# Which last convolutions wait for the last mixing, and in which order an inverse transform emits its steps

## The chip, the cores and the metric

The kernel runs on one core of one Trainium2 chip. The metric is device time in microseconds (us) of one execution; a lower number is better. All arithmetic is float32 (a few transforms split a float32 number into two reduced-precision parts and add the two products).

## The reference

The input is `x` of shape (4, 64, 256, 256): 4 batches, 64 channels, images of 256 x 256. Four layers run one after the other:

- Layers 0, 1 and 3 are the same kind of layer, a long convolution per channel plus a scaled copy of the input: `y = irfft2(rfft2(x) * k_f)[:256, :256] + x * bias`. The filter of a channel is an outer product of one vector along the rows and one along the columns (`k = einsum('ijk,imk->ijmk', hx, hy)`), so a two-dimensional convolution is two one-dimensional ones, and each of these is a product with a triangular Toeplitz matrix.
- Layer 2 is a Haar wavelet layer:

```python
f1 = haar2d(x)
for i in range(2):
    f3 = f1 * v[i]
    f4 = einsum('bchw,oc->bohw', f3, conv_w[i])   # mixes the 64 channels
    acc = acc + sign(f4) * relu(abs(f4) - tau[i])
y = haar2d(acc, inverse=True) + x
```

The mixing needs all 64 channels of a batch; everything else works on one channel alone.

## The kernel before

**The work of one batch** falls into three parts, and each has a function in the kernel.

1. `convolutions(b, ticks)`: for each channel, the convolutions of layers 0 and 1 (tiles `a0`, `y0`, `a1`, `y1`) and then the forward Haar transform along rows and columns (`sd`, `pz`, `co`). The coefficients go to memory as `coef`, and the input of the wavelet layer is saved as `keep`. A *contraction* (`contract`, lines 167 and 168) multiplies a 256 x 256 image with a triangular Toeplitz matrix; it appears as four matmuls in the code and eight in the trace. A convolution takes two contractions: the first into bank `pa`, copied by ScalarE to `a` (`first`, line 176), the second into bank `py`, where VectorE adds the bias term and writes `y` (`second`, line 189).
2. `mixing(b, start, n_act)`: 64 groups `g`. Each loads four rows of coefficients of all channels, mixes the channels on TensorE (`px`, line 308), scales (`f`, lines 325 and 327), shrinks (`mag`, lines 333, 335 and 340) and adds into `z` (line 344).
3. `inverse(b, start, put_off)`: for each channel `c`, one tick apart, `fetch` loads the saved `keep` as `r` (line 359) and lets ScalarE gather the channel out of `z` as `zc` (line 361); `rows` makes four matmuls into bank `pw` (lines 368 and 369), then ScalarE rounds (`w`, line 371) and VectorE takes the rest (line 372); `cols` makes the column transform into bank `pu` (line 381), then VectorE adds `r` (`t`, line 385) and unpacks the pairs (`u`, lines 388 and 389). `u` is the input of layer 3. The *last convolution* of a channel is layer 3: `first`, `second` and the write to the output (`last`, line 403).

**Order of the work.** The kernel does not run these functions one after the other. Each stage of each unit is noted with `at(tick, place, run, unit)`; at the end all notes are sorted by tick, then by place, then by the order of noting, and called in that order. A scheduler below may still shift an instruction by a few places, above all loads. On each engine the instructions then stand in one order. `stream` gives stage `s` of a unit the tick `tick + s` and the place `-s`, so that within a tick a later stage (of an earlier unit) comes first.

**How the parts lie beside each other.** The mixing of batch `b` runs for 67 ticks beside `convolutions(b + 1)`, whose 64 units are spread evenly over it (`spread`). Then the inverse of batch `b` runs for 64 ticks beside the rest of those convolutions. Batch 3 has no next batch, so its mixing would have nothing beside it. Therefore the third batch (`b == B - 2`) is treated differently: its inverse computes no last convolution but writes `u` to memory (`late`), and `convolution(2, ticks)` loads the 64 images again beside the last mixing and computes the last convolutions there. And 20 of the 64 units of `convolutions(3)` are moved from the third mixing into the third inverse:

```python
            ticks = spread(ahead, end + 2)
            if b == B - 2:
                ticks = spread(ahead, end, 44) + spread(end, end + 49, 20)
```

**Buffers.** All banks `pa`, `py`, `pw`, `pu`, `pz` come from one pool of four in PSUM (`psm`); the Toeplitz tiles `t` from a pool of five; `u` and `y0` share a pool of three (`y`); `y3`, the final result of a channel, and `co` share one of two; `r` and the mixing's `f` share one of three. Loads and the write of `coef` are issued on SyncE (SP), the writes of `keep`, `late` and the output on ScalarE's queue.

Of the kernel before, what the change touches and what calls it, by code (L numbers as in the profile page):

```python
# [9 lines left out]
F32 = mybir.dt.float32  # L10
# [6 lines left out]
B, C, S, EMB, ORD = 4, 64, 256, 33, 64  # L17
P = 128
# [19 lines left out]
def conv_seq_kernel(ctx, tc, x, fz, fw, bias, decay, haar, haar_row, factors, vt, taut, wmix, out):  # L38
# [14 lines left out]
    nc = tc.nc  # L53

    const = ctx.enter_context(tc.tile_pool(name="const", bufs=1))
    dram = ctx.enter_context(tc.tile_pool(name="dram", bufs=1, space=DRAM))
# [93 lines left out]
    sd = zpool.tile([P, 8, 2, 2, P], F32, name="sd")  # L150
    keep = [dram.tile([C, P, 2, 2, P], F32, name=f"keep{b}") for b in range(B)]
    coef = [dram.tile([2, C, P, S], F32, name=f"coef{b}") for b in range(B)]
    late = dram.tile([C, P, 2, S], F32, name="late")

    def toeplitz(layer, c, name):

        t = tp.tile([P, 2, S], F32, name=name, tag="toep")
        nc.sync.dma_start(t, ap(pads[layer], c * 2 * ROW, [[1, P], [ROW, 2], [1, S]]))
        return t
# [45 lines left out]
    def at(tick, place, run, unit):  # L205
        events.append((tick, place, len(events), run, unit))

    def stream(stages, ticks):

        for unit, tick in enumerate(ticks):  # L210
            for s, stage in enumerate(stages):
                if stage is not None:
                    at(tick + s, -s, stage, unit)

    def convolutions(b, ticks, in_parts=False):

        st = {}

        def load(c):
            xt = io.tile([P, 2, S], F32, name=f"x_{b}_{c}", tag="in", bufs=4)  # L220
            nc.sync.dma_start(xt, x[b, c].rearrange("(k p) w -> p k w", p=P))
            st[c] = {"x": xt, 0: toeplitz(0, c, f"t0_{b}_{c}")}

        last_second = second(b, st, "a1", 1, "y0", "y1", "res")

        def pairs(c):
            last_second(c)
            v = st.pop(c)["y1"].rearrange("p k (w e) -> p k w e", e=2)
            t = sd[:, c % 8]
            nc.vector.tensor_add(t[:, :, 0, :], v[:, :, :, 0], v[:, :, :, 1])  # L230
            nc.vector.tensor_sub(t[:, :, 1, :], v[:, :, :, 0], v[:, :, :, 1])  # L231
            nc.scalar.dma_start(keep[b][c], t)

        def levels(steps):
            def run(n):
                t = sd[:, n % 2 * 4 : n % 2 * 4 + 4]
                for step in steps:
                    v = t[:, :, :, 0, :].rearrange("p c k (w e) -> p (c k) w e", e=2 * step)
                    even, odd = v[:, :, :, 0], v[:, :, :, step]
                    nc.vector.tensor_sub(odd, even, odd)  # L240
                    nc.vector.scalar_tensor_tensor(even, even, 2.0, odd, ALU.mult, ALU.subtract)

            return run

        parts = {}

        def split(c):

            w = parts[c] = mx.tile([P, 2, 2, S], F32R, name=f"sp_{b}_{c}", tag="f4")
            t = sd[:, c % 8].rearrange("p k e w -> p k (e w)")  # L250
            nc.scalar.copy(w[:, 0], t)
            nc.vector.tensor_tensor(w[:, 1], t, w[:, 0].bitcast(F32), ALU.subtract)

        def down(c):
            ps = bank(f"pz_{b}_{c}")
            flat = "p k w -> p (k w)"
            if in_parts:
                for i in range(2):
                    nc.tensor.matmul(
                        ps.rearrange(flat), hbr, parts[c][:, i].rearrange(flat), start=(i == 0), stop=(i == 1)  # L260
                    )
            else:
                nc.tensor.matmul(
                    ps.rearrange(flat), hbt, sd[:, c % 8].rearrange("p k e w -> p (k e w)"), start=True, stop=True
                )
            t = io.tile([P, 2, S], F32, name=f"co_{b}_{c}", tag="co", bufs=BUFS["co"])
            nc.scalar.copy(t, ps)
            nc.sync.dma_start(coef[b][:, c].rearrange("k p w -> p k w"), t)

        stream(  # L270
            [load, first(b, st, "x", 0, "a0"), second(b, st, "a0", 0, "x", "y0", "y", ahead=1), first(b, st, "y0", 1, "a1"), pairs],
            ticks,
        )
        for n in range(C // 4):
            end = ticks[4 * n + 3] + 4
            for s, steps in enumerate([(1,), (2, 4), (8, 16, 32, 64)]):
                at(end + 1 + s, 1, levels(steps), n)
            for j in range(4):
                if in_parts:
                    at(end + 3 + j, 2, split, 4 * n + j)  # L280
                at(end + 4 + j, 2, down, 4 * n + j)
        return ticks[-1] + 11
# [68 lines left out]
    def inverse(b, start, put_off):  # L351

        st = {}

        def fetch(c):
            if c == 0:
                butterfly(b)
            r = mx.tile([P, 2, 2, P], F32, name=f"r_{b}_{c}", tag="f", bufs=3)
            nc.sync.dma_start(r, keep[b][c])
            a = mx.tile([P, 2, 2, P], F32, name=f"zc_{b}_{c}", tag="mag")  # L360
            nc.scalar.copy(a, z[:, :, :, c].rearrange("p h (i k) -> p h k i", k=2))  # L361
            st[c] = {"r": r, "z": a}

        def rows(c):
            a = st[c]["z"]
            ps = psm.tile([P, 2, 2, P], F32, name=f"pw_{b}_{c}", tag="mm")
            for m in range(2):
                nc.tensor.matmul(ps[:, m, 0, :], a[:, 0, m, :], hsinv, start=True, stop=True)  # L368
                nc.tensor.transpose(ps[:, m, 1, :], a[:, 1, m, :], ident)  # L369
            w = mx.tile([P, 2, 2, 2, P], F32R, name=f"w_{b}_{c}", tag="f4")  # L370
            nc.scalar.copy(w[:, 0], ps)  # L371
            nc.vector.tensor_tensor(w[:, 1], ps, w[:, 0].bitcast(F32), ALU.subtract)
            st[c]["w"] = w
            if not put_off:
                st[c][2] = toeplitz(2, c, f"t2_{b}_{c}")

        def cols(c):
            ps = psm.tile([P, 2, 2, P], F32, name=f"pu_{b}_{c}", tag="mm")
            flat = "p m e w -> p (m e w)"
            for i in range(2):  # L380
                nc.tensor.matmul(  # L381
                    ps.rearrange(flat), hb, st[c]["w"][:, i].rearrange(flat), start=(i == 0), stop=(i == 1)
                )
            t = io.tile([P, 2, 2, P], F32, name=f"t_{b}_{c}", tag="res", bufs=BUFS["res"])
            nc.vector.scalar_tensor_tensor(t, st[c]["r"], 0.5, ps, ALU.mult, ALU.add)  # L385
            u = io.tile([P, 2, S], F32, name=f"u_{b}_{c}", tag="y", bufs=BUFS["y"])
            v = u.rearrange("p m (w e) -> p m w e", e=2)
            nc.vector.tensor_add(v[:, :, :, 0], t[:, :, 0, :], t[:, :, 1, :])
            nc.vector.tensor_sub(v[:, :, :, 1], t[:, :, 0, :], t[:, :, 1, :])
            st[c]["u"] = u  # L390

        stages = [None, fetch, rows, cols]
        if put_off:
            stages.append(lambda c: nc.scalar.dma_start(late[c], st.pop(c)["u"]))
        else:
            stages += last(b, st)
        stream(stages, range(start - 1, start - 1 + C))

    def last(b, st):
        return [  # L400
            first(b, st, "u", 2, "a3"),
            second(b, st, "a3", 2, "u", "y3", "co"),
            lambda c: nc.scalar.dma_start(out[b, c].rearrange("(k p) w -> p k w", p=P), st.pop(c)["y3"]),
        ]

    def convolution(b, ticks):

        st = {}

        def load(c):  # L410
            u = io.tile([P, 2, S], F32, name=f"v_{b}_{c}", tag="in", bufs=4)
            nc.sync.dma_start(u, late[c])
            st[c] = {"u": u, 2: toeplitz(2, c, f"t2_{b}_{c}")}

        stream([load, *last(b, st)], ticks)


    def spread(begin, end, n=C):
        return [begin + i * (end - begin - 1) // (n - 1) for i in range(n)]

    groups = S // 4
    ready = convolutions(0, range(C), in_parts=True)
    ahead = C
    start = ready + 3
    for b in range(B):
        mixing(b, start, 8 if b + 1 < B else 6)
        end = start + groups + 3
        if b + 1 < B:
            ticks = spread(ahead, end + 2)
            if b == B - 2:  # L430
                ticks = spread(ahead, end, 44) + spread(end, end + 49, 20)
            ready = convolutions(b + 1, ticks)
        else:
            convolution(b - 1, spread(start - 2, end + 2))
        inverse(b, end, put_off=b == B - 2)

        start = max(end + C, ready + 3)
        ahead = start - 3
# [112 lines left out]
```

## Time and profile before

| | us |
|---|---|
| three runs | 3121.33, 3124.04, 3125.69 |
| median | 3124.04 |
| the profiled execution, its own time | 3127.37 |
| its span in the profile | 3125.6 |

| stretch of the profile (us from the start) | length, us |
|---|---|
| filters, then the convolutions of batch 0 | 486.0 |
| mixing 0 from its first `f` to its last `z`, then inverse 0 (486.0 to 1190.4) | 704.4 |
| mixing 1, inverse 1 (1190.4 to 1944.5) | 754.1 |
| mixing 2, inverse 2 (1944.5 to 2587.7) | 643.2 |
| mixing 3, inverse 3 (2587.7 to 3125.6) | 537.9 |

A stretch begins with the first scaling (`f`, line 325) of its mixing. The granted TensorE clock is 0.996 of full speed in the mean, so the clock hardly plays a part. In the profile PE is the matmuls of TensorE, PEld its weight loads, DVE is VectorE, ACT is ScalarE. [...] neighbours overlap in the record; what an instruction costs TensorE is the distance from its start to the next one's start.

### The profile page before, as it was taken

Reading aid. Unit: us, or ns where it says so; the run is one execution under the profiler, and the core shown is the slowest. Engines: PE = TensorE matmul, PEld = TensorE weight load, DVE = VectorE, ACT = ScalarE, POOL = GpSimd, SP = SyncE. Lnnn points to the kernel's source line nnn. Section 1 sums busy time; section 2 is a strip of 40 time slices with the busy share of each in tenths; the row PEclk is TensorE's granted clock in tenths of the full one; section 3 lists DMA queues with packets and bytes.
Section 4 is the critical chain, followed back from the end, with each engine's and each line's share of the span. In section 5 each row is a group of like instructions: output and inputs, shape, how many; then the busy total and the mean of one; then the engine's idle time right before and its main releaser. Section 6 shows DMA issues by size and latency. Waiting matters only on the chain. (4 is left out here: it accounts for less than half of the span.)

```text
span 3125.6 us, 50721 instructions
## 1 busy us (share of the span) xinstructions
PE 3010.4 (96%) x16944; PEld 2622.0 (84%) x16944; DVE 2526.0 (81%) x4453; ACT 1923.9 (62%) x4054; POOL 0.2 (0%) x4
## 2 busy tenths in 40 slices
PE   5999999999999999999999999999998989999999
PEld 3999988888888998888888899888887768888998
DVE  6676668989986777988887676999987889998776
ACT  1333336777765555766675555778774557887554
POOL 0000000000000000000000000000000000000000
PEclk9999999999999999999999999999999999999999
DMA  4778776666667776666666777666667877886776
GB/s 121 218 228 233 230 228 205 202 195 188 199 200 217 211 210 188 196 204 194 203 201 207 217 211 203 190 187 186 191 206 232 254 241 236 239 232 210 211 211 180
DMA packets 555864, 649.82 MB, mean 208 GB/s; under 512 B 39793, under 2 KB 440532, under 8 KB 555476
## 3 DMA queue, kind: packets, MB, share of 16 engines
q1 hardware_dynamic: 439460, 493.44, 55.8%
q10 hardware_dynamic: 116144, 153.13, 13.6%
q8 instruction: 137, 2.24, 0.3%
q14 instruction: 123, 1.01, 0.1%
HBM read 426.67 MB, written 219.74 MB: 207 GB/s over the span
## 5 line engine op out<-in xcount | busy, mean ns | idle before, releaser
L167 PE MATMUL py<-t,a 128*128 128x256 f32 x3072 | 927.4, 384 | 25.5 <-ACT a L176 23.9
L176 ACT COPY a<-pa 128x512 f32<-128x512 f32 x768 | 458.6, 598 | 603.7 <-PE pa L168 487.1
L168 PEld LDWEIGHTS py<-t,a 128*128 128x128 f32 x3072 | 584.1, 190 | 79.4
L327 ACT ACTIVATE f<-px,vt 128x64 f32<-128x64 f32 x1920 | 424.2, 331 | 299.8 <-DVE f L325 292.0
L167 PEld LDWEIGHTS py<-t,a 128*128 128x128 f32 x3072 | 486.6, 191 | 128.8 <-issue 64.5
L168 PE MATMUL py<-t,a 128*128 128x128 f32 x3072 | 590.5, 274 | 0.0
L308 PE MATMUL px<-wb,f 128*128 128x256 f32 x2048 | 496.1, 380 | 5.4 <-ACT f L327 3.6
L308 PEld LDWEIGHTS px<-wb,f 128*128 128x128 f32 x2048 | 365.1, 191 | 46.3 <-ACT f L327 6.2
L385 DVE SCALAR_TENSOR_TENSOR t<-r,pu 128x512 f32<-128x512 f32 x256 | 175.9, 687 | 213.9 <-PE pu L381 207.4
L167 PE MATMUL pa<-t,y 128*128 128x256 f32 x1024 | 310.0, 385 | 27.3 <-DVE y L189 26.5
L335 DVE TENSOR_TENSOR mag<-mag,vt 128x1024 f32<-128x1024 f32 x256 | 312.3, 1220 | 29.4 <-ACT mag L333 27.6
L167 PE MATMUL pa<-t,x 128*128 128x256 f32 x1024 | 307.1, 382 | 8.6 <-DMA t<-pad 8.6
L340 DVE SCALAR_TENSOR_TENSOR mag<-mag,f 128x1024 f32<-128x1024 f32 x256 | 311.7, 1217 | 0.8
L333 ACT ACTIVATE mag<-f 128x1024 f32<-128x1024 f32 x256 | 283.8, 1108 | 9.6 <-DVE z L344 6.5
L361 ACT COPY zc<-z 128x512 f32<-128x512 f32 x256 | 282.0, 1103 | 8.0 <-DVE z L199 6.5
L334 ACT ACTIVATE f<-f 128x1024 f32<-128x1024 f32 x256 | 272.1, 1063 | 10.7 <-DVE sd L231 3.5
L371 ACT CAST w<-pw 128x512 fp32r<-128x512 f32 x256 | 150.1, 586 | 196.7 <-PE pw L369 177.3
L189 DVE SCALAR_TENSOR_TENSOR y<-y,bsb,py 128x512 f32<-128x512 f32 x256 | 190.2, 743 | 90.3 <-PE py L168 90.0
L189 DVE SCALAR_TENSOR_TENSOR y<-x,bsb,py 128x512 f32<-128x512 f32 x256 | 190.3, 743 | 53.4 <-PE py L168 53.3
L167 PE MATMUL pa<-t,u 128*128 128x256 f32 x768 | 229.7, 381 | 1.9 <-PE py L168 1.0
L168 PEld LDWEIGHTS pa<-t,x 128*128 128x128 f32 x1024 | 195.4, 191 | 26.7
L168 PEld LDWEIGHTS pa<-t,y 128*128 128x128 f32 x1024 | 195.3, 191 | 26.7
(65 smaller groups left out, 4342.9 us busy)
## 6 DMA issues: line engine op xcount, KB each, us to landing
t<-pad SPq DMA_DIRECT2D x768, 256.0 KB, 3.9
x<-in_x SPq DMA_DIRECT2D x256, 256.0 KB, 3.9
keep<-sd ACTq DMA_DIRECT2D x256, 256.0 KB, 3.2
coef<-co SPq DMA_DIRECT2D x256, 256.0 KB, 2.9
f<-coef SPq DMA_DIRECT2D x256, 256.0 KB, 3.8
r<-keep SPq DMA_DIRECT2D x256, 256.0 KB, 3.0
out_y<-y ACTq DMA_DIRECT2D x256, 256.0 KB, 3.6
late<-u ACTq DMA_DIRECT2D x64, 256.0 KB, 3.6
```

The lines of the kernel that those rows point to most:

```text
L167: nc.tensor.matmul(ps[:, m, :], src[:, 0, m * P : (m + 1) * P], t[:, ::-1], start=True, stop=False)
L168: nc.tensor.matmul(ps[:, m, P:], src[:, 1, m * P : (m + 1) * P], t[:, : P - 1 : -1], start=False, stop=True)
L176: nc.scalar.copy(a, ps)
L189: nc.vector.scalar_tensor_tensor(y, s[res], bsb[:, layer, c : c + 1], ps, ALU.mult, ALU.add)
L308: nc.tensor.matmul(ps[:, h, q, :], f[:, q, h * P : (h + 1) * P], wb.rearrange("p r n -> p (r n)"), start=True, stop=True,)
L327: nc.scalar.mul(f4[:, j], px[:, j], scale(g, 0)[:, j : j + 1])
L333: nc.scalar.activation(mag, f4, AF.Abs)
L334: nc.scalar.activation(f4, f4, AF.Sign)
L335: nc.vector.tensor_sub(mag, mag, over(g, 1, 16))
L340: nc.vector.scalar_tensor_tensor(mag, mag, 0.0, st[g]["f4"], ALU.max, ALU.mult)
L361: nc.scalar.copy(a, z[:, :, :, c].rearrange("p h (i k) -> p h k i", k=2))
L385: nc.vector.scalar_tensor_tensor(t, st[c]["r"], 0.5, ps, ALU.mult, ALU.add)
```

## The change

- `put_off` is no longer a yes or no for a whole batch but a set of channels: 2, 5, 8, ... 62, which is 21 of 64. In the inverses of batches 0, 1 and 2 these 21 channels write `u` to `late`; the other 43 make their last convolution in place. `late` grows to hold all batches.
- Beside the last mixing, `convolution` now computes 63 last convolutions, 21 of each of the first three batches, instead of 64 of the third.
- The 64 units of `convolutions(3)` are spread over the third mixing as in the batches before; none is left for the third inverse.
- The stages of an inverse get places of their own. Within a tick the order was: write, `second`, `first`, `cols`, `rows`, `fetch`. It becomes: `rows` (-9), `cols` (-8), `first` (-7), `second` (-6), write (-5), then the convolution and mixing stages of the tick, with `fetch` at place -1 among them. The ticks of the stages stay as they are. This holds for all four inverses, the last one too, which puts nothing off.

```diff
-    late = dram.tile([C, P, 2, S], F32, name="late")
+    late = dram.tile([B, C, P, 2, S], F32, name="late")
...
-            if not put_off:
+            if c not in put_off:
                 st[c][2] = toeplitz(2, c, f"t2_{b}_{c}")
...
-        stages = [None, fetch, rows, cols]
-        if put_off:
-            stages.append(lambda c: nc.scalar.dma_start(late[c], st.pop(c)["u"]))
-        else:
-            stages += last(b, st)
-        stream(stages, range(start - 1, start - 1 + C))
+        ends = last(b, st)
+        for c in range(C):
+
+            at(start + c, -1, fetch, c)
+            at(start + c + 1, -9, rows, c)
+            at(start + c + 2, -8, cols, c)
+            if c in put_off:
+                at(start + c + 3, -5, lambda c: nc.scalar.dma_start(late[b, c], st.pop(c)["u"]), c)
+            else:
+                for s, stage in enumerate(ends):
+                    at(start + c + 3 + s, s - 7, stage, c)
...
-    def convolution(b, ticks):
-
-        st = {}
-
-        def load(c):
-            u = io.tile([P, 2, S], F32, name=f"v_{b}_{c}", tag="in", bufs=4)
-            nc.sync.dma_start(u, late[c])
-            st[c] = {"u": u, 2: toeplitz(2, c, f"t2_{b}_{c}")}
-
-        stream([load, *last(b, st)], ticks)
+    def convolution(which, ticks):
+
+        for (b, c), tick in zip(which, ticks):
+            st = {}
+
+            def load(c, b=b, st=st):
+                u = io.tile([P, 2, S], F32, name=f"v_{b}_{c}", tag="in", bufs=4)
+                nc.sync.dma_start(u, late[b, c])
+                st[c] = {"u": u, 2: toeplitz(2, c, f"t2_{b}_{c}")}
+
+            for s, stage in enumerate([load, *last(b, st)]):
+                at(tick + s, -s, stage, c)
...
+    put_off = range(2, C, 3)
...
-            ticks = spread(ahead, end + 2)
-            if b == B - 2:
-                ticks = spread(ahead, end, 44) + spread(end, end + 49, 20)
-            ready = convolutions(b + 1, ticks)
+            ready = convolutions(b + 1, spread(ahead, end + 2))
         else:
-            convolution(b - 1, spread(start - 2, end + 2))
-        inverse(b, end, put_off=b == B - 2)
+            convolution(
+                [(i, c) for i in range(B - 1) for c in sorted(put_off)], spread(start - 2, end + 2, (B - 1) * len(put_off))
+            )
+        inverse(b, end, put_off if b + 1 < B else ())
```

## The prediction

> **What bounds the kernel now.** The page's first part comes first, then its slices.
>
> ```profile
> PE 3010.4 (96%) x16944; PEld 2622.0 (84%) x16944; DVE 2526.0 (81%) x4453; ACT 1923.9 (62%) x4054; POOL 0.2 (0%) x4
> ...
> PE   5999999999999999999999999999998989999999
> ...
> DMA  4778776666667776666666777666667877886776
> ```
>
> TensorE is the bound nearly everywhere; its share dips at slices 31 and 33. The window sums say which stage that is: mixing 1, inverse 1, mixing 2, inverse 2, mixing 3, inverse 3, in this order.
>
> ```profile
> 1190.40:1661.80 471.40, 463.68 (x2485) 398.30 (x2484) 414.19 (x691) 323.49 (x808) 0.00 (x0) 1.00 0.66 197
> 1661.80:1944.50 282.70, 282.19 (x1746) 253.96 (x1746) 196.06 (x373) 151.66 (x216) 0.00 (x0) 1.00 0.71 212
> 1944.50:2324.10 379.60, 368.24 (x1930) 312.16 (x1929) 357.24 (x569) 298.26 (x761) 0.00 (x0) 1.00 0.64 191
> 2324.10:2587.70 263.60, 231.08 (x1287) 189.82 (x1285) 203.04 (x433) 140.48 (x201) 0.00 (x0) 0.96 0.76 242
> 2587.70:2867.30 279.60, 271.48 (x1458) 239.42 (x1457) 274.33 (x321) 242.15 (x572) 0.00 (x0) 1.00 0.79 233
> 2867.30:3125.60 258.30, 249.78 (x1586) 228.81 (x1584) 176.47 (x324) 140.88 (x195) 0.00 (x0) 1.00 0.68 198
> ```
>
> The columns are length, then busy time of PE, PEld, DVE and ACT, clock, DMA share, GB/s. Only inverse 2 leaves TensorE idle by a lot (231 of 264 busy, weight loads 190). The waits inside it name the cause:
>
> ```profile
> PE pa L167 <- DVE y L189: 20.2, 14, 4.3
> PE pu L381 <- DVE w L372: 5.1, 7, 3.0
> PE pu L381 <- ACT w L371: 2.6, 6, 0.7
> ```
>
> Last, the timeline in the middle of inverse 0 shows one tick:
>
> ```profile
> 1063.62 0.69 DVE L385 SCALAR_TENSOR_TENSOR t<-r,pu 128x512 f32<-128x512 f32 x1 [1.01 <-PE pu L381]
> ...
> 1064.08 0.60 PE L167 MATMUL py<-t,a 128*128 128x256 f32 x2
> ...
> 1064.34 0.59 ACT L371 CAST w<-pw 128x512 fp32r<-128x512 f32 x1 [0.54 <-PE pw L369]
> 1064.34 0.43 DVE L388 TENSOR_TENSOR u<-t 128x256 f32<-128x256 f32 x1
> ...
> 1065.02 0.68 DVE L372 TENSOR_TENSOR w<-pw,w 128x512 fp32r<-128x512 f32 x1
> ...
> 1065.39 0.60 PE L167 MATMUL pa<-t,u 128*128 128x256 f32 x2
> ...
> 1067.17 0.38 PE L368 MATMUL pw<-hrow,zc 128*128 128x128 f32 x2
> ```
>
> From start to start, py takes 1.31 us (1064.08 to 1065.39), pa 1.31, pu 0.47, and pw, which began at 1063.42, 0.66. The sum is 3.75, and the starts of `t` are 3.75 apart through the middle of inverses 0, 1 and 3: no gap on TensorE. In the same way px costs 1.73 (1500.12 to 1501.85) and pz 0.86 (1515.24 to 1516.10). I call these slots.
>
> [...] in inverse 2 PE counts 231 us busy, while the slots worked out below fill about 200 of 263.6. [...] here batches 0 and 1 are TensorE-bound throughout and inverse 2 is not. [...] a pa that waits for `y` holds every matmul behind it. So the order of emission matters.
>
> **How much TensorE idles in each batch.** Per batch: 64 units of layers 0 and 1, each 4 x 1.31 + 0.86 = 6.10, make 390; mixing 64 x 1.73 = 111; rows and cols 64 x 1.13 = 72; 64 last convolutions at 2.62 make 168. Batch 1: 741 of 754.1, so 13 idle. Batch 2, without the 168: 573 of 643.2, so **70 idle**. It is in inverse 2: 72 for rows and cols and 20 x 6.1 = 122, some 200 with the first late units, against 263.6. Mixing 3: 64 x (1.73 + 2.62) = 278 of 279.6, full.
>
> **The change part by part.** Total work hardly alters: 63 put-off channels instead of 64, one `late` write and one read less. The gain can only be idle time of inverse 2, minus idle time that the thinner inverses 0, 1 and 2 get.
>
> *Inverses 0, 1, 2: the group of three channels.* In the built order (the listing of each engine's instructions, no times) a steady group is on TensorE: pw20 pu19 pa18, pw21 pu20 pa19 py18, pw22 pu21 py19. Slots: 3 x 1.13 + 4 x 1.31 = 8.63, against 11.25 now. DVE has, back to back, w 0.60, t 0.72, u 2 x 0.34, y 0.66: 3 x 2.00 + 2 x 0.66 = 7.3. ACT: 3 copies zc 1.10, 3 w 0.59, 2 a 0.59: 6.3. TensorE still bounds, but some waits have less cover. Latencies from the timeline: pw's last slot to ACT w 0.26, w 0.59, DVE 0.09 later; pu's slot to `t` 0.20; `u`'s end to pa 0.05 to 0.1. With pw20's slot ending at 0:
>
> - DVE w20 runs from 0.94 to 1.54, then t19 and u19 (built order) to 3.02. So pa19 may start at 3.1; TensorE arrives after pu19 0.47, pa18 1.31, pw21 0.66, pu20 0.47 = 2.91: about 0.2 lost.
> - t20 3.15, w21, u20, y18 (py18 ends near 5.7) to 6.6, t21 near 7.05, w22 7.8, u21 done 9.1; pa21 is due at 9.3: nothing lost.
> - pu20, pu21, pu22 want w at 1.7, 4.7, 8.5 and come later. The four banks are free in time: pw22 needs w21 (4.6) and comes at 5.7. zc22 stands on ACT behind w20 and ahead of a18, so it is ready well before pw22.
>
> The group takes 8.85, a gain of 2.4. Of the 21 put-off channels four (2 to 11) fall in the first twelve ticks, where the tail of the next batch's convolutions makes ticks of 4 to 7 us and TensorE is full: 2.62 each. The sum: 17 x 2.4 + 4 x 2.62 = **51 us less per batch** in batches 0 and 1. Bounds: 55 (pure slots) and 0 (a tick stays at 3.75).
>
> *Batch 2* then becomes a batch like batch 1: 754 - 51, less about 4, because two late units rather than three convolution units start just before the following mixing (3 first contractions and their successors, some 8 us, against 4): 699 in place of 643.2, **+56**. Inside: mixing 2 goes from 380 to about 471, inverse 2 from 264 to about 230.
>
> *Mixing 3*: one unit less, **-3**.
>
> *DMA.* A put-off channel drops the Toeplitz load from SP and writes `late` instead of the output on ACT's queue; the last mixing reloads it. Per group SP issues 5 loads instead of 6 and ACT 3 writes as before: 8 x 0.262 MB in 8.85 us, 237 GB/s; inverse 2 moved 242 and mixing 3 233, so I cost it at 0. `late` lands 3.7 us after issue (2.0 to 6.3); the buffer of u20 is wanted again by u23, about 13 us after pw20 while the write lands near 9.4. With a landing 4 us later it would stall.
>
> *Order of places.* In inverse 3 all four steps remain, 3.75 of slots per tick; DVE fills 2.66 of them. Cost 0, cover: TensorE itself. From below nothing is to be had (no gap now); from above see the slower rival.
>
> **Sum.** -51 - 51 + 56 - 3 = -49. The profiled execution took 3127.4, 3.3 above the median, so 3078 for its like, or 3075 against the median of 3124.0. I take **3076**.
>
> **The rivals.**
>
> 1. *Thinner ticks cost more than worked out, but less than they save.* Waits through DVE in its strict order make the group 9.2 to 9.65 instead of 8.85. For it: inverse 2 now has waits of just this kind. Against it: those stand in the old order, with py first, and ticks without convolution there run in 2.0 us, DVE's own time. At 9.3 a batch saves 17 x 1.95 + 10.5 = 44, the total is 3124 - 88 + 63 - 3 = 3096; at 9.65, 38 and 3124 - 75 + 69 - 3 = 3115.
> 2. *No gain that can be told*, within 0.2% or 6.2 us (about what a measurement of this kernel can tell from no change): the group at 9.7 to 9.95: 37 to 33 saved per batch, 3118 to 3130, by the same sum.
> 3. *Slower, through zc.* `fetch` is noted as the last inverse step of a tick and `rows` as the first of the next. If the gather zc (1.10 on ACT) only starts after a of the same tick, TensorE waits: pw 0.66 + pu 0.47 + pa 1.31 + 0.26 + 0.59 + 1.10 = 4.4 for each tick that has a pa, and 2.9 for the others. A group is 11.7, nothing is saved, and inverse 3 loses 64 x 0.65 = 42. Total, with 0 saved per batch: 3124 + (754 - 4 - 643) - 3 + 42 = 3270. It turns slower from a group of 9.8 on. Against it: in the built order zc stands half a tick earlier in all four inverses (w30, zc32, a28 in the last).
> 4. *More gain*: the group at pure slots, 8.63, and the 13 us of other idle time partly filled: 3124 - 110 + 52 - 3 = 3063, or a little under.
>
> That the change doesn't do what it says is excluded by the built order: 63 `late` writes, 21 per inverse.
>
> **How the numbers follow.** The likeliest case (group 8.63 to 9.2, 3060 to 3095) has 0.70, rival 4 below it 0.05, rival 1 0.08, rival 2 0.06, the slower side 0.11. Below 0.2% faster: 0.70 + 0.05 + 0.08 = 0.83. The range 3055 to 3112 takes in the likeliest case, most of rival 4 and half of rival 1.
>
> **What would show it.** After: window sums with mixing 2 near 471 and inverses 0 to 2 near 230 each; starts of `t` that repeat in groups of three, 8.85 apart; the wait of pa for `u` (DVE L389) near 0.2 per group, so 3 to 5 us per inverse; starts of `t` in the last inverse still 3.75 apart; PE slices without the dip. Wrong would be: groups above 9.8; pw waiting for zc; `u` waiting for `late`; mixing 3 longer than 280.

## The result and the profile after

The changed kernel took **3086.3 us** (median of 4 runs, 3085.62 to 3091.79) against 3122.7 for the kernel before beside it (4 runs, 3121.33 to 3125.69): ratio 0.9886, 95% interval 0.9869 to 0.9903. That is 36 us less; 48 less were forecast, and 3086.3 lies inside the forecast range. The profiled execution took 3091.79, with a span of 3090.0.

First the page's busy times and two rows of its 40 slices, for the kernel after:

```profile
PE 3004.4 (97%) x16944; PEld 2615.3 (85%) x16944; DVE 2523.4 (82%) x4453; ACT 1926.9 (62%) x4054; POOL 0.2 (0%) x4
...
PE   5999999999999999999999999999999999999999
...
DMA  4777877666667876666667776666667777877676
```

The instruction counts are those of before, so no work was taken away. The two 8s in TensorE's row are gone. The window sums of the kernel after, for inverse 0, mixing 1, inverse 1, mixing 2, inverse 2, mixing 3 (this window runs 2 us past its last `z`) and inverse 3:

```profile
912.70:1147.30 234.60, 229.60 (x1401) 200.51 (x1400) 177.55 (x350) 139.33 (x194) 0.00 (x0) 1.00 0.76 228
1147.30:1612.00 464.70, 458.31 (x2459) 394.07 (x2459) 411.52 (x688) 323.30 (x807) 0.00 (x0) 1.00 0.67 199
1612.00:1855.50 243.50, 238.62 (x1441) 207.50 (x1439) 180.69 (x356) 141.46 (x197) 0.00 (x0) 0.99 0.75 226
1855.50:2319.90 464.40, 457.98 (x2449) 393.19 (x2450) 411.41 (x688) 322.50 (x806) 0.00 (x0) 1.00 0.67 199
2319.90:2555.70 235.80, 230.32 (x1401) 200.38 (x1400) 179.42 (x355) 139.74 (x195) 0.00 (x0) 1.00 0.77 230
2555.70:2839.20 283.50, 275.06 (x1474) 241.41 (x1472) 275.83 (x323) 242.76 (x574) 0.00 (x0) 1.00 0.79 231
2839.20:3090.00 250.80, 246.66 (x1576) 227.28 (x1576) 175.32 (x323) 141.13 (x195) 0.00 (x0) 1.00 0.67 202
```

Inverse 2 is now busy on TensorE for 230 of 236 us, where it was 231 of 264, and it holds more matmuls (1401 records, before 1287): the idle time is filled. The third batch's mixing and inverse look like those of the second. By the starts of the mixings, in us:

| stage | before | after | difference | forecast |
|---|---|---|---|---|
| up to mixing 0 | 486.0 | 485.0 | -1.0 | 0 |
| batch 0 | 704.4 | 662.3 | -42.1 | -51 |
| batch 1 | 754.1 | 708.2 | -45.9 | -51 |
| batch 2 | 643.2 | 700.2 | +57.0 | +56 |
| batch 3 | 537.9 | 534.3 | -3.6 | -3 |

The sum is -35.6; the own times of the two profiled executions differ by the same (3127.4 and 3091.8). What was bought and where it was paid for is as forecast; batches 0 and 1 gave less. All stages here and below come from one profiled execution of each kernel. That of the kernel after is the slowest of its four, 5.5 us above their median, so a difference of one or two us between the stages of two kernels says little.

The group of three channels: the starts of `t` (line 385) on VectorE in inverse 0 of the kernel after.

```profile
1034.50 0.68 DVE L385 SCALAR_TENSOR_TENSOR t<-r,pu 128x512 f32<-128x512 f32 x1
...
1036.12 0.69 DVE L385 SCALAR_TENSOR_TENSOR t<-r,pu 128x512 f32<-128x512 f32 x1
...
1040.10 0.69 DVE L385 SCALAR_TENSOR_TENSOR t<-r,pu 128x512 f32<-128x512 f32 x1 [0.38 <-PE pu L381]
...
1043.35 0.68 DVE L385 SCALAR_TENSOR_TENSOR t<-r,pu 128x512 f32<-128x512 f32 x1
```

Three channels take 1.62 + 3.98 + 3.25 = **8.85 us**, the 8.85 of the forecast; they took 11.25. On TensorE's timeline of the same ticks one sees where most of the 0.2 above the pure slots is lost:

```profile
1035.38 0.71 PE L381 MATMUL pu<-w,hb 128*128 128x512 f32 x2
1036.08 0.67 PE L167 MATMUL pa<-t,u 128*128 128x256 f32 x2
...
1041.79 0.70 PE L381 MATMUL pu<-w,hb 128*128 128x512 f32 x2
1042.33 0.59 PE L167 MATMUL pa<-t,u 128*128 128x256 f32 x2
```

From a pu to the pa behind it are 0.70 us the first time and 0.54 the second. The first pa is the one whose `u` was forecast late, by about 0.2; the excess is 0.16, and the list of waits doesn't name it here.

TensorE's largest waits in inverse 2 of the kernel after (us in total, times, longest):

```profile
PE pz L263 <- DVE sd L241: 1.9, 1, 1.9
PE pz L263 <- DVE w L372: 1.4, 1, 1.4
PE py L167 <- DVE y L189: 0.6, 2, 0.4
```

Of the 20.2 us of pa behind `y`, 0.4 are left. The new name is pz, the Haar matmul down the columns that ends a unit of the next batch's convolutions (`down`, line 263). It reads `sd`, which VectorE's `levels` (line 241) write.

The timeline of inverse 1 shows two places where other work stands behind such a wait. TensorE stands still for 3.44 us ahead of a pz (until 1674.18), and the pu whose `w` VectorE ended at 1672.13 starts at 1677.00, behind this pz and the pw that follows it. VectorE stands still for 1.55 us ahead of a `y` (until 1670.67), and the step of `levels` whose input was written by 1667.85 starts at 1671.33, behind this `y`.

### The profile page after: what moved, and what is told of

It is laid out like the page before. It is cut to its first block, busy times and chain, and to the rows that moved or that the text cites. A ratio compares the mean times of both kernels' runs of the same rounds, so it can differ in the third digit from the quotient of the medians.

```text
span 3090.0 us, 50474 instructions
## 1 busy us (share of the span) xinstructions
PE 3004.4 (97%) x16944; PEld 2615.3 (85%) x16944; DVE 2523.4 (82%) x4453; ACT 1926.9 (62%) x4054; POOL 0.2 (0%) x4
## 3 DMA queue, kind: packets, MB, share of 16 engines
q1 hardware_dynamic: 439316, 493.18, 56.5%
## 5 line engine op out<-in xcount | busy, mean ns | idle before, releaser
L167 PE MATMUL py<-t,a 128*128 128x256 f32 x3072 | 926.0, 383 | 27.9 <-ACT a L176 24.6
L189 DVE SCALAR_TENSOR_TENSOR y<-u,bsb,py 128x512 f32<-128x512 f32 x193 | 143.8, 745 | 102.4 <-PE py L168 98.7
```

The source lines that it names most:

```text
L167: nc.tensor.matmul(ps[:, m, :], src[:, 0, m * P : (m + 1) * P], t[:, ::-1], start=True, stop=False)
L189: nc.vector.scalar_tensor_tensor(y, s[res], bsb[:, layer, c : c + 1], ps, ALU.mult, ALU.add)
```

## The experiments

Ratios are to runs of the kernel before beside them (3121.4 to 3122.1 us). Diffs are against the kernel after, or against the one named. Theory: the gain is TensorE's idle time of inverse 2, spent on last convolutions of batches 0 to 2, and a group of three ticks costs what TensorE's slots cost only if `u` is formed early in the tick.

### The old order within a tick (old_places)

```diff
-            at(start + c + 1, -9, rows, c)
-            at(start + c + 2, -8, cols, c)
+            at(start + c + 1, -2, rows, c)
+            at(start + c + 2, -3, cols, c)
...
-                at(start + c + 3, -5, lambda c: nc.scalar.dma_start(late[b, c], st.pop(c)["u"]), c)
+                at(start + c + 3, -4, lambda c: nc.scalar.dma_start(late[b, c], st.pop(c)["u"]), c)
...
-                    at(start + c + 3 + s, s - 7, stage, c)
+                    at(start + c + 3 + s, -4 - s, stage, c)
```

> The changed kernel with one part undone: the stages of an inverse get their former places within a tick (fetch -1, rows -2, cols -3, first -4, second -5, write -6). Theory (the order carries a large part, because thin ticks need cover for two chains): in the built order a group of three channels is pw py pu, pw pa pu, pw py pa pu. pu needs w, which comes 1.7 us after pw, and a lone py covers 1.3 of it: 0.4 lost. A pa without a py ahead of it needs u, 1.75 after pu, and pw covers 0.66: 1.1 lost. The group takes 8.63 + 1.5 = about 10.1 instead of 8.84, an inverse 17 x 1.3 = 21 us more, the kernel about 3086 + 64 = 3150: slower than before the change. Rival (the gain is TensorE work moved out of the thin stage, the order is not needed): groups stay within 0.2 of 8.84, the time within 3080 to 3095.

Measured: 3148.1 us (3146.1 to 3148.2), ratio 1.0079 (1.0064 to 1.0094). The groups take 2.68 + 3.63 + 3.75 = 10.06 instead of 8.85. TensorE's waits in the whole run:

```profile
PE pa L167 <- issue: 68.2, 56, 1.8
PE py L167 <- ACT a L176: 24.7, 33, 1.5
```

The second line is no effect of the order: the kernel after has it too (24.6 us, 35 times). "issue" says only that the profile names no releaser. The timeline of TensorE at one of these 56 places:

```profile
1046.41 0.50 PE L381 MATMUL pu<-w,hb 128*128 128x512 f32 x1
...
1047.08 0.27 PE L369 MATMUL pw<-hrow,zc 128*128 128x128 f32 x1
1048.53 0.45 PE L167 MATMUL pa<-t,u 128*128 128x256 f32 x1 [1.18 <-issue]
```

VectorE's timeline at the same place names it:

```profile
1046.27 0.74 DVE L189 SCALAR_TENSOR_TENSOR y<-u,bsb,py 128x512 f32<-128x512 f32 x1
1046.95 0.69 DVE L385 SCALAR_TENSOR_TENSOR t<-r,pu 128x512 f32<-128x512 f32 x1
1047.67 0.43 DVE L388 TENSOR_TENSOR u<-t 128x256 f32<-128x256 f32 x1
1048.01 0.42 DVE L389 TENSOR_TENSOR u<-t 128x256 f32<-128x256 f32 x1
```

`u` ends at 1048.43 and pa starts at 1048.53: it waited for `u`. The kernel after has the same 0.10 us from the end of `u` to a pa at 48 places, one in each of 16 groups of inverses 0, 1 and 2 (1035.98 to 1036.08 in the group shown above). VectorE was not late: `t` starts at 1046.95, 0.04 us after the last matmul of pu ends (1046.41 + 0.50). What is missing is cover on TensorE: where no py stands ahead of a pa, only the four matmuls of pw separate it from the pu that its `u` comes from, as the expectation has it. In the new order pa18, pw21 and pu20 stand between pu19 and pa19. So without the new places the same put-off channels make the kernel slower than before. The rival, that the order plays no part, falls. The new places alone, with no channel put off, were not run; the last inverse, which puts nothing off, shows below what they are worth there.

### The third batch spread, its 64 channels still put off, in the old order (third_all_old)

Against the kernel before, this is one edit:

```diff
-            ticks = spread(ahead, end + 2)
-            if b == B - 2:
-                ticks = spread(ahead, end, 44) + spread(end, end + 49, 20)
-            ready = convolutions(b + 1, ticks)
+            ready = convolutions(b + 1, spread(ahead, end + 2))
```

> The kernel before with one part of the change done: the 64 convolutions of batch 3 are spread over the third mixing as in the other batches; the third batch still puts off all its 64 last convolutions, the first two none, and the places are the old ones. Theory (idle time of TensorE in inverse 2 is a matter of how thin its ticks are): mixing 2 takes about 471 us like mixing 1; inverse 2 has 12 ticks with the tail of the convolutions, some 60 us, and then 52 ticks at 2.0, VectorE's own time per tick, 104 us. Batch 2 takes 471 + 165 = 636 in place of 643, the kernel about 3116: most of the gain of the change is not here. Rival (the 20 convolutions in the third inverse were the whole trouble, the spreading of put-off channels is not needed): batch 2 takes 573 of matmul slots and about 30 idle, the kernel about 3085.

Measured: 3124.1 us (3119.7 to 3130.2), ratio 1.0008 (0.9999 to 1.0016): no difference. Batch 2 took 644 us, 8 more than expected; its inverse ran at half clock for 6.8 and 3.4 us, in which TensorE was busy for 8, so the clock explains at most 4 of them. Its mixing, its inverse and a stretch of that inverse:

```profile
1937.60:2406.00 468.40, 462.56 (x2483) 397.88 (x2482) 413.67 (x690) 323.47 (x808) 0.00 (x0) 1.00 0.66 199
2406.00:2581.90 175.90, 146.52 (x737) 106.48 (x735) 149.33 (x313) 115.62 (x153) 0.00 (x0) 0.97 0.78 246
2470.00:2570.00 100.00, 81.01 (x403) 55.10 (x403) 96.36 (x197) 81.12 (x103) 0.00 (x0) 1.00 0.83 261
```

All convolutions now lie in mixing 2, which is full, and the inverse is short, but there VectorE is busy 96 of 100 us and TensorE's weight loads fill 55. Moving the convolutions alone only moves the idle time; with all of one batch's channels put off, VectorE sets ticks of 2.0 us. The rival, that spreading the convolutions of batch 3 is the whole gain (3085), falls: the put-off channels have to be spread over the batches too. The same with the new places was not run; with VectorE busy 96 of 100 us there was little for another order to win.

### How many channels: every fourth, every second

```diff
-    put_off = range(2, C, 3)
+    put_off = range(2, C, 4)
```

> The changed kernel with every fourth channel put off (2, 6, 10, ... 62): 16 per batch, 48 in the last mixing instead of 63. Theory (mixing 3 is held by VectorE as much as by TensorE: per group f 0.82, two passes over mag 1.13 each, z 0.60, and y 0.66 for each late unit): inverses 0 to 2 take 4 x 2.4 = 10 us more each, mixing 3 takes 64 x 3.69 + 48 x 0.66 = 268 instead of 281; the kernel about 3086 + 29 - 13 = 3102. Rival (mixing 3 is held by TensorE alone): it takes 64 x 1.73 + 48 x 2.62 = 237, the kernel about 3071.

Measured: 3102.9 us (3101.9 to 3104.2), ratio 0.9936 (0.9921 to 0.9951), as expected in sum. Mixing 3, with 48 late convolutions beside it, took 275.9, not the 268 of the theory and far from the 237 of TensorE alone:

```profile
2576.10:2852.00 275.90, 241.99 (x1250) 210.38 (x1248) 269.23 (x308) 236.92 (x559) 0.00 (x0) 1.00 0.68 197
```

VectorE is busy 269 of 276. With 15 convolutions fewer than in the kernel after, mixing 3 is 5.4 us shorter, 0.36 each, while TensorE is idle for 34 us of it: VectorE sets its length here.

```diff
-    put_off = range(2, C, 3)
+    put_off = range(1, C, 2)
```

> The changed kernel with every second channel put off: 32 per batch, 96 in the last mixing instead of 63. Theory (the number put off is right when the last mixing is just filled): TensorE alone holds mixing 3, 64 x 1.73 + 96 x 2.62 = 362 instead of 281, 81 us more. In the inverses a pair of ticks takes 1.62 + 3.25 = 4.87, as seen where put-off channels stand two apart; 26 pairs after the twelfth tick make 127 instead of 150 us, 24 less per batch. The kernel about 3086 - 72 + 81 = 3095. Rival (thin ticks so close together wait on VectorE's strict order): a pair takes 5.5, the kernel about 3140.

Measured: 3082.0 us (3077.2 to 3082.6), ratio 0.9867 (0.9852 to 0.9882): 13 below the theory's 3095, and far from the rival's 3140. Batches 0 to 2 took 633.1, 674.6 and 678.0, which is 29, 34 and 22 less than with every third (24 each expected). Mixing 3, with 96 late convolutions, took 348.1 (362 expected):

```profile
2470.00:2818.10 348.10, 345.55 (x1911) 306.48 (x1912) 301.41 (x350) 262.74 (x600) 0.00 (x0) 1.00 0.85 249
```

Here TensorE is full (346 of 348), and the late convolutions are paid for in time: 67 us more than with 63, 2.0 each. So somewhere above 63 mixing 3 passes from VectorE to TensorE. The ratio's interval overlaps that of every third.

### Which channels: none in the first twelve ticks (from_twelve, twelve_again)

The group of three gave what was forecast, so channels 2, 5, 8 and 11 were the first suspects. The start of inverse 0 in the kernel before and in the kernel after:

```profile
913.00:974.00 61.00, 60.08 (x344) 50.93 (x343) 41.88 (x89) 29.54 (x45) 0.00 (x0) 1.00 0.73 215
913.00:971.00 58.00, 53.26 (x302) 44.28 (x301) 38.64 (x86) 28.92 (x43) 0.00 (x0) 1.00 0.70 212
```

TensorE was full there before (60 of 61 us) and isn't any more (53 of 58). The same number of channels, 21 per batch, from 12 on:

```diff
-    put_off = range(2, C, 3)
+    put_off = [12 + i * 50 // 20 for i in range(21)]
```

> The changed kernel with other put-off channels: 21 again, but none of the first twelve (12, 14, 17, 19, 22, ... 62, one in 2.5). Theory (the four put-off channels among the first twelve gain next to nothing, because there the tail of the next batch's convolutions rules): the first twelve ticks take as long as in the changed kernel or up to 4 us longer, and each of the four is worth up to 2.4 us later on; 5 to 7 us less per inverse, the kernel about 3068. Rival (every put-off channel costs some idle time wherever it stands): the first twelve ticks take 10 us longer, the total stays within 3082 to 3092.

Measured: 3068.6 us (3062.3 to 3070.7), ratio 0.9822 (0.9808 to 0.9837). Batches 0 to 2 took 655.2, 698.2 and 691.1. The starts of `t` repeat over five ticks, 3.25 + 1.63 + 3.25 + 1.62 + 3.98 = 13.73 against 18.75, so a put-off channel saves 2.51 us. The first twelve intervals between starts of `t`, summed, took 59.1, 58.1 and 58.2 us in inverses 0 to 2, and 54.9, 57.0 and 56.5 in the kernel after: its four early channels saved 4.2, 1.1 and 1.7 us there, not 10.5. (This profiled execution is the fastest of its four, 6.3 us below their median; that of twelve_again is at its median and has 656.5, 699.0 and 692.4 for the batches and 58.8, 58.4 and 58.8 for the twelve intervals.)

The same kernel once more, beside a later run:

> The kernel of from_twelve once more, for a comparison of second_late on the same chip: 3062 to 3071.

Measured: 3065.5 us (3062.8 to 3068.3), ratio 0.9816 (0.9802 to 0.9829).

### Why the early channels save little (pz_later)

In the kernel after, between 1612 and 1690 us (the start of inverse 1), TensorE has this wait:

```profile
PE pz L263 <- DVE sd L241: 3.4, 1, 3.4
```

In the whole run it has three of them, 7.7 us. As the ticks get thinner, pz comes before VectorE's `levels` are done. Here the last eight pz of a batch come a tick later:

```diff
+            off = 1 if n >= C // 4 - 2 and not in_parts else 0
...
-                at(end + 4 + j, 2, down, 4 * n + j)
+                at(end + 4 + off + j, 2, down, 4 * n + j)
```

> The changed kernel with one edit outside the inverse: the column transforms pz of the last eight channels of the batches 1 to 3 are noted one tick later. Theory (part of what the early put-off channels fail to gain is TensorE held in its strict order by a pz that waits for VectorE's levels, 2 to 3.6 us in each inverse): that wait goes, 2 to 3 us less per inverse, the kernel about 3079. Rival (that wait is taken over by the next instruction of the tail, since VectorE is late as a whole): no difference, 3083 to 3090.

Measured: 3081.5 us (3080.5 to 3084.2), ratio 0.9870 (0.9855 to 0.9885); the interval overlaps that of the kernel after. The same window of this kernel:

```profile
PE pa L167 <- ACT co L267: 1.3, 1, 1.3
PE py L167 <- DVE y L189: 0.2, 1, 0.2
```

The wait is gone, a smaller one has come, and the three batches are 2.1, 3.0 and 1.3 us shorter. The first twelve intervals save 2.8, 4.5 and 2.6 us, and the next 48 give 1.0, 1.6 and 2.3 of that back. In inverse 1 the clock has a part in it: right behind the wait of 3.4 us the kernel after ran at half clock for 3.4 us (from 1674.4), which can be worth 1.7; pz_later did not. So the pz that wait for VectorE's `levels` explain some 2 of the 6 to 9 us that are missing per inverse. That rests on the stages and waits of one execution each, since the ratios alone don't separate the two kernels. What holds the rest is open.

### Less of the scaling on VectorE in the last mixing (twelve_seven)

If VectorE sets mixing 3, moving one of its columns of scaling to ScalarE should help. Against from_twelve:

```diff
-        mixing(b, start, 8 if b + 1 < B else 6)
+        mixing(b, start, 8 if b + 1 < B else 7)
```

> from_twelve with one edit more: in the last mixing ScalarE scales 7 of the 16 parts of a group instead of 6. Theory (VectorE and TensorE hold mixing 3 together, VectorE slightly more): VectorE has 0.066 us less per group, mixing 3 falls from 280.5 to TensorE's 64 x 1.73 + 63 x 2.62 = 276 at best, the kernel 3 to 4 us below from_twelve. Rival (ScalarE becomes the one that is waited for): mixing 3 takes 281 or more, no gain.

Measured: 3084.8 us (3083.3 to 3086.9), ratio 0.9882 (0.9865 to 0.9898): 16 slower than from_twelve. The window of mixing 3 in from_twelve:

```profile
2526.80:2807.30 280.50, 272.96 (x1465) 240.23 (x1464) 274.70 (x320) 242.29 (x572) 0.00 (x0) 1.00 0.80 231
```

The same window here:

```profile
2528.10:2824.70 296.60, 278.04 (x1454) 243.18 (x1453) 276.37 (x322) 250.47 (x635) 0.00 (x0) 0.97 0.74 217
```

TensorE's wait for the scaling on ScalarE in mixing 3, in from_twelve:

```profile
PE px L308 <- ACT f L327: 4.3, 7, 0.8
```

And here:

```profile
PE px L308 <- ACT f L327: 16.5, 8, 2.4
```

In the two profiled executions, which are 21 us apart, mixing 3 has 16 us of this and the start of inverse 3 another 4. TensorE's wait for ScalarE's `f` grew by 12 us; the rival, that ScalarE comes to be waited for, holds, although ScalarE is busy only 250 of 297. Within mixing 3 the clock was also halved in five stretches of 3.4 us, worth 8.5 us at most. One of them:

```profile
2571.00:2574.00 3.00, 3.00 (x11) 2.55 (x11) 2.56 (x4) 2.46 (x8) 0.00 (x0) 0.50 0.01 3
```

12 and 8.5 together would cover the 20 us, but no run separates the waits from the clock.

### More channels, none early (second_late)

```diff
-    put_off = range(2, C, 3)
+    put_off = range(14, C, 2)
```

> The changed kernel with the put-off channels 14, 16, 18, ... 62: 25 per batch, none of the first twelve, 75 in the last mixing. Theory (a put-off channel gains most where they stand two apart and after the twelfth tick): each saves 7.50 - 4.87 = 2.6 us, 25 of them 66 us per batch, where from_twelve has 21 at 2.51, 53 us; 13 less per batch, and mixing 3 takes 12 x 2.62 = 31 us more. The kernel 5 to 10 us below from_twelve. Rival (pairs pay for thin ticks now and then, as the odd ticks of 2.0 to 2.7 in every_second show, and mixing 3 takes the rest back): the same as from_twelve within 4 us, or slower.

This puts off 25 channels per batch, 75 in all. Measured: 3061.8 us (3060.7 to 3062.5), ratio 0.9804 (0.9791 to 0.9818), 3.8 below twelve_again on the same chip; the runs of the two don't overlap, the intervals of the ratios do. Batches 0 to 2 took 643.6, 687.6 and 685.9, less than in twelve_again by 13, 11 and 6.5 (13 each expected); mixing 3 took 299.7, which is 19 more, and inverse 3 6.6 more. In this mixing 3 TensorE is busy 295 us and VectorE 287, so at 75 TensorE is already the fuller one. This is the best version found: 60 us below the kernel before, 25 below the kernel after.

## Why the prediction was right in kind and too large by some 12 us

- **Where the idle time lies: right.** Inverse 2 holds more matmuls than before in 28 us less. In third_all_old the idle time stays when the put-off channels stay in one batch.
- **The group of three: right**, 8.85 us. The late `u` costs 0.16 of the 0.2 forecast per group; the list of waits doesn't show it as was forecast, it shows 0.5 once.
- **The term that was mis-sized is "4 x 2.62"** for the early channels. That TensorE is full in the first twelve ticks was read rightly. That it would stay full, so that a removed convolution gives back its whole slots, was not: the starts of `t` divide the batches more finely, and show it. The table has us less than before; batch 2 is set against batch 1 of before, as in the forecast.

  | stretch | batch 0 | batch 1 | batch 2 | forecast |
  |---|---|---|---|---|
  | first `f` of the mixing to the first `t` | 0.3 | 8.3 | 8.4 | 0 |
  | the first twelve intervals | 4.2 | 1.5 | 2.0 | 10.5 |
  | the next 48, sixteen groups | 38.6 | 38.5 | 38.5 | 38.4 |
  | from there to the next first `f` | -0.9 | -2.3 | 5.2 | 2.4; batch 2: 6.4 |

  The early channels fall short by 6.3, 9.0 and 8.5 us, in all three batches. Part of it is the chain through VectorE's `levels` and pz (pz_later); the rest is open. The seventeenth group, of channel 62, doesn't lie among the others but at the end of the inverse, and gave nothing there in batches 0 and 1.
- **Batch 2 came to 700 us, 699 was forecast: in part luck.** It misses as much on its early channels as the others do. The 8 us that its mixing and first steps are shorter make up for it, and they were not forecast. In part they are a matter of where a stage ends: in the kernel before the first `f` of mixing 1 came 7.5 us ahead of the last `t` of inverse 0, now it comes 0.6 us behind it.
- **"One unit less, -3" in mixing 3: the number came, from elsewhere.** Mixing 3 took 281.3 us, where the same measure gives 279.1 before (both to the end of the last `z`); "longer than 280" was named as a sign of error, and it is one. VectorE sets its length, as every_fourth shows, so one convolution less frees next to nothing. The last batch still fell by 3.6, and that is the new order, which was put at nothing: from the last `z` of mixing 3 to the last instruction it takes 255.8 us before, 254.5 in old_places and 249.9 in the kernel after. Old_places differs from the kernel after by the order alone, and its last batch takes 537.7 us, as before. With the new order inverse 3 begins with shorter ticks (2.43 and 3.75 us instead of 4.24 and 5.06).
- **Left out: the clock in inverse 2 of before.** The kernel before ran at half clock in three stretches there, of 6.8, 3.4 and 10.2 us. Three windows, the first with the full clock ahead of a stretch:

```profile
2340.00:2349.00 9.00, 6.93 (x42) 5.77 (x40) 6.45 (x14) 3.23 (x5) 0.00 (x0) 1.00 0.78 236
2349.00:2356.00 7.00, 4.80 (x17) 4.25 (x18) 5.17 (x16) 2.15 (x3) 0.00 (x0) 0.51 0.45 153
2557.50:2567.00 9.50, 4.30 (x9) 2.60 (x10) 6.32 (x20) 1.90 (x3) 0.00 (x0) 0.50 0.43 138
```

  TensorE was busy for some 13 of these 20 us, so at half clock at most 6 of the 70 us idle in batch 2 were slow matmuls rather than gaps. They began at gaps of TensorE of 4.3, 2.05 and 3.0 us and went away with these in inverse 2 (the kernel after has one stretch of 3.4 us, in inverse 1), so the sum was not hurt.
- **DMA at nothing: right.** It moved 231 GB/s in mixing 3 and 226 to 230 in inverses 0 to 2, and none of TensorE's larger waits names the reloaded `late`. In the middle of inverse 3 `t` starts 3.75 apart, before and after, so there the new order cost nothing.
- **The rivals.** Thin ticks that cost 9.2 to 9.65 per group, or 9.7 and more, did not come, nor did pw waiting for zc. (In rival 3 the 2.9 us of a tick without pa doesn't come out of its own terms, 4.4 less 1.31 being 3.1; its group would be 11.9 instead of 11.7, with nothing saved either way.) The measured time lies between the forecast and rival 1, but through another term. The slower side was real in one respect: old_places shows that a group of 10.06, past the 9.8 that was named as the turning point, does make the kernel slower (3148).

## What to carry to other kernels

Work that may be done late is best taken evenly from stages that one engine fills: taken all from one stage, it leaves that stage to the next engine (in third_all_old to VectorE, busy for 96 of 100 us), and taken where another chain follows closely it gives back little, here 1 to 4 us for four convolutions worth 10.5. When ticks are thinned, what the bound engine needs next must be emitted early enough to have other work of that engine between: the same work in another order was 62 us slower. Moving goes on paying until the stage that receives the work is full on its own bound; here mixing 3 grew by 5 us from 48 to 63 late convolutions, by 19 for the next 12 (twelve_again to second_late), and by 48 for the 21 after those.

## What was not expected of the hardware

- TensorE's clock was halved (0.50) in stretches of 3.4, 6.8 and 10.2 us, in these runs all multiples of 3.4. In inverse 2 of the kernel before they began 2.1 us into a gap of TensorE of 4.3 us (at 2349.0), 1.1 us behind a gap of 2.05 (at 2396.8) and 0.1 us into a gap of 3.0 (at 2557.2); three other gaps there, of 2.19, 2.05 and 2.08 us, were followed by none. In the kernel after the one stretch began 0.2 us behind a gap of 3.4 us, and a gap of 2.4 us in inverse 0 (from 966.9) was followed by none. In mixing 3 of twelve_seven, with its five stretches, the longest wait of TensorE was 2.4 us. So a gap of two us or more can have a stretch at it or none; what decides is not shown.
- A wait for VectorE can stand under "issue": in old_places, whose list has 68.2 us of pa under that name, the pa whose timeline is shown waits for `u` and starts 0.10 us after its end.
